# Attention of a two-layer block in the order of a list scheduler, without the repeated products at its begin

## The chip, the core and the metric

The kernel runs on one core of a Trainium2 chip. The core has TensorE (PE, matrix products into PSUM), VectorE (DVE), ScalarE (ACT), GpSimd (POOL) and SyncE (SP, which here only issues DMAs). Each engine works through its own queue in order; semaphores join them. The metric is the device time of one execution in microseconds, the median of the runs shown.

## What is computed

The reference is a two-layer block on x of shape 16 x 128 x 32 x 32, all in float32. The change touches layer 0 alone: linear attention, then the input side of a spectral filter.

```python
# --- layer 0 ---
x = x + _L0_conv_ref(_ln_c(x), ...)            # linear attention over 1024 tokens, 4 heads
t = _to_tokens(x)
t = t + _L0_ffn_ref(_ln_t(t), ...)             # causal FFT convolution with 16 filters, and taps
x = _from_tokens(t, x)
# --- layer 1: convolution block, then routed experts ---
...
# inside the attention:
q = softmax(q, over tokens) * SCALE
k = softmax(k, over channels of a head)
context = einsum('bhdc,bhec->bhde', k, v)
out = einsum('bhde,bhdc->bhec', context, q)
# inside the filter, per sample: three taps
out = out + einsum('btd,de->bte', u shifted by i, Mu[i])
```

## The kernel before

The 16 samples of x, 512 KB each, pass through the core in stages. The first, lines 221 to 774, is the attention stage; the second (L777 on) generates transfer matrices and multiplies spectra; then come layer 1's convolution and experts. Only the attention stage is edited.

**One sample in the attention stage** is some sixty named steps, methods of the class `Attention` (L356 on). In order of dependence:

- `tokens` (L367): issues the load of sample b + 2, then eight PE transposes of x into a PSUM tile. `moments` (L378, statistics on DVE at L135), `tokens_copy` (L374, ACT), `variance`, `root` (ACT: logarithm and exponential, L121 and L122), `scales` (one Newton step on DVE, L127 to L129, and the shift, L390), `norm` (L407, eight ACT operations at L144), `spread`, `group`, `group_var`, `group_root`, `group_scale` for the group norm.
- `channels` (PE transposes back, L172), `channels_copy` (ACT, gives xn), `q_` and `k` (PE, L433 and L451), the two softmaxes (`q_max`, `k_max`, `k_sub`, `k_sum` on DVE; `q_exp`, `k_exp` on ACT; `k_scale` on POOL, L476), `q_tokens`, `q_copy`, `context` (L499), `context_mask`, `fold` and `fold2` with their copies, `out` (L534), `out_add` (DVE, L539, adds to x).
- `input` (L543, PE transposes of the new x at L157), `moments2`, `input_copy` (ACT, L550, gives ub), `variance2`, `root2`, `scales2`, `norm2` (ACT, L144), then three users of ub: `even` and `odd` (PE, L571: half of the spectrum each) and `taps_in` (PE, L172). Behind `even` and `odd` stand ACT copies (L245, L247), DVE sums (L254 to L267) and POOL butterflies (L285 to L309), the last of them in `odd_turns4` (L625), which also issues the spectrum's write to DRAM (`vd`, L628). Behind `taps_in` stand `taps_copy` (ACT, gives u), `taps` (L633, twelve products at L639) and `taps_add` (L645, DVE at L646), which issues the write of x (`xd`, L647).

A float32 product appears in the profile as two PE instructions, a transpose as one.

**Set-up work** is woven in. `filters` (L649) makes the filters' spectra (`ph`) out of `phi` and `wf` (products at L657) and mixes sixteen 512 KB pieces `mi` into `mst` on DVE (L686, L688). `prepare` (L692) scales convolution weights on POOL.

**PSUM.** All 1024-column tiles come from `big()` (L343), three buffers in turn: a step that opens one waits until the third-last has been read. Small ones come from the tag `s`, two buffers.

**What sets the order.** PE, DVE, ACT and POOL run exactly in the order of the program text (`manual_schedule` with `PINNED`, L46 and L759); SP is not pinned in this stage. The order is written out by hand: the tuple `period` (L742) lists the steps with how many periods each runs behind `taps_in`; the loop over p (L760) goes through it once per period for 16 + 6 periods, so that steps of up to seven samples are interleaved. `filters` and `prepare` are generators that advance one piece per period.

**Repeated products.** `keep` (L159) multiplies the identity by itself into an unused tile. In this stage the table `idle` (L354) places 5, 4, 1 and 2 of them at the begin of the program.

**Planner.** `planned` (L1783) is a list scheduler that the layer-1 stage already uses: from a table of steps (engine, cost in us, due time, what it depends on, which buffers it opens and closes) it makes one order. Among the steps that can start within 0.25 us of the earliest, it takes the one with the earliest due time.

**After the stage** (L873 on, SP pinned too) four reads `xc` of chunk 0 (L793) feed POOL's `turns` (L808, L809), `generate` (L817) and its copies `g` on DVE and ACT (L828, L830), then `multiply` (L841).

## Time and profile before

| | us |
|---|---|
| median of 3 runs (lowest, highest) | 1227.47 (1225.88, 1232.86) |
| the profiled execution, device time | 1229.05 |
| its span, first to last instruction | 1227.0 |
| first product on x (PE, L152) | 7.53 |
| start of the first, eleventh and last `taps` | 87.54, 303.55, 378.78 |
| end of the last spectrum's butterflies (POOL) | 386.66 |
| first full run of products at L841 | 399.54 |

| busy in the span | us | share |
|---|---|---|
| PE | 1155.2 | 94% |
| DVE | 932.7 | 76% |
| ACT | 721.2 | 59% |
| POOL | 602.2 | 49% |

The page's groups give, for each line and engine, the count of instructions, their busy time and mean, and the idle time in front of them with what ended most of it. The answers on waits put that idle time down to pairs of lines. The chain of waits goes back from the last instruction, at each step to what released it. A matmul's end is modelled and overlaps the next one, so work on PE is best read from the distance between starts. The mean granted clock of TensorE was 0.988.

### The profile page before, as it was taken

To read this page: it belongs to the slowest core of one execution; us is meant where nothing else is said; L and a number is where in the kernel's file an instruction comes from. 1 tells how busy PE (TensorE), PEld (TensorE's weight loads), DVE (VectorE), ACT (ScalarE), POOL (GpSimd) and SP (SyncE) were. 2 spreads that over 40 slices of the span, in tenths; PEclk is the share of its full clock that TensorE was granted. 3 is DMA by queue.
4 is the path that set the end of the run, shared out by engine and by line. 5 is a ranking of instruction groups with operands and counts; after the bars stand their busy time and mean duration, and the time that the engine had idled before them with its cause. 6 is when DMAs were issued, how large, how long until landed. Compare 5 with 4: busy or idle time off the path is not lost.

```text
span 1227.0 us, 34351 instructions
## 1 busy us (share of the span) xinstructions
PE 1155.2 (94%) x14364; PEld 946.8 (77%) x14364; DVE 932.7 (76%) x1956; ACT 721.2 (59%) x1414; POOL 602.2 (49%) x800
## 2 busy tenths in 40 slices
PE   6889999999999999999997999999999999998996
PEld 4677767777677899998996888888888888885453
DVE  5888888887767677777764689898888989877335
ACT  4777777776656777877760445555555555554211
POOL 2436454664568788888882433343333333230003
PEclk9999999999999999999998999999999999999998
DMA  7004435243446244344348511233233322416998
GB/s 283 24 31 158 133 99 173 87 160 124 132 142 182 81 141 139 137 139 140 125 147 282 134 52 52 87 103 120 80 121 112 103 86 70 155 35 237 357 404 341
DMA packets 91243, 175.14 MB, mean 143 GB/s; under 512 B 5968, under 2 KB 42064, under 8 KB 90448
## 3 DMA queue, kind: packets, MB, share of 16 engines
q1 hardware_dynamic: 90448, 170.46, 41.1%
q0 software_dynamic: 640, 2.49, 0.6%
q8 instruction: 113, 1.85, 0.6%
q14 instruction: 42, 0.34, 0.1%
HBM read 110.28 MB, written 62.65 MB: 141 GB/s over the span
## 4 chain that ended last, share of the span: by engine, by line
PE 52%; DVE 22%; issue 10%; ACT 5%; DMA 5%; POOL 5%; SPq 0%; POOLq 0%; DVEq 0%; ACTq 0%
PE pcv L1013 10%; PE py L841 8%; PE pg L817 8%; PE big L639 6%; DVE bst L135 4%; PE big L172 3%; PE big L152 3%; PE big L571 3%; PE big L451 2%; PE big L534 2%; PE big L433 2%; DVE abss L1256 1%; DVE xp L1278 1%; DVE xp L1140 1%; POOL v L808 1%
## 5 line engine op out<-in xcount | busy, mean ns | idle before, releaser
L1013 PE MATMUL pcv<-v,cw 128*128 128x256 f32 x1152 | 258.2, 380 | 1.6 <-POOL v L1203 1.6
L1013 PEld LDWEIGHTS pcv<-v,cw 128*128 128x128 f32 x1152 | 214.7, 190 | 34.7 <-issue 4.9
L828 DVE COPY g<-pg 128x512 f32<-128x512 f32 x196 | 127.6, 682 | 67.9 <-PE pg L817 67.9
L830 ACT COPY g<-pg 128x512 f32<-128x512 f32 x316 | 161.1, 606 | 28.7 <-PE pg L817 27.9
L817 PE MATMUL pg<-ph,mst 32*128 32x128 f32 x4096 | 138.9, 278 | 1.4 <-DVE x L646 0.9
L817 PEld LDWEIGHTS pg<-ph,mst 32*128 32x128 f32 x4096 | 125.9, 187 | 15.6 <-DVE g L828 8.3
L841 PE MATMUL py<-g,v 128*32 128x128 f32 x4096 | 126.0, 276 | 1.9 <-POOL v L809 1.6
L841 PEld LDWEIGHTS py<-g,v 128*32 128x32 f32 x4096 | 109.2, 110 | 9.7 <-POOL v L809 2.1
L144 ACT ACTIVATE tok<-tok,sts 128x128 f32<-128x128 f32 x256 | 101.9, 480 | 16.9 <-DVE sts L1090 13.6
L135 DVE BATCH_NORM_STATS2 bst<-big 128x6 f32<-128x256 f32 x252 | 89.6, 416 | 19.9 <-PE big L152 10.7
L808 POOL TENSOR_TENSOR v<-xc 128x256 f32<-128x256 f32 x128 | 98.0, 790 | 9.9 <-DMA xc<-vd 9.2
L639 PE MATMUL big<-u,mu 128*128 128x128 f32 (+4 forms) x384 | 86.0, 380 | 0.0
L1203 POOL TENSOR_TENSOR v<-abss 128x256 f32<-128x256 f32 x64 | 49.1, 787 | 68.2 <-DVE abss L1199 56.8
L287 POOL TENSOR_TENSOR xf<-ab 128x256 f32<-128x256 f32 x34 | 24.8, 728 | 112.6 <-DVE ab L254 112.5
L1222 POOL TENSOR_TENSOR yo<-abss 128x256 f32<-128x256 f32 x32 | 23.5, 734 | 107.5 <-DVE abss L1218 107.5
L639 PEld LDWEIGHTS big<-u,mu 128*128 128x128 f32 x384 | 56.7, 191 | 18.0 <-issue 15.4
L571 PE MATMUL big<-wf,ub 128*128 128x256 f32 x256 | 63.5, 392 | 0.2
L809 POOL TENSOR_SCALAR v<-v 128x256 f32<-128x256 f32 x64 | 55.0, 860 | 5.6
L476 POOL TENSOR_TENSOR ke<-ke,ks 128x1024 f32<-128x1024 f32 x16 | 30.6, 1913 | 54.9 <-DVE qs L484 43.2
L144 ACT ACTIVATE tt<-tt,sts 128x128 f32<-128x128 f32 x120 | 47.8, 481 | 13.9 <-DVE sts L1090 13.9
L571 PEld LDWEIGHTS big<-wf,ub 128*128 128x128 f32 x256 | 47.0, 193 | 9.1 <-ACT xn L424 3.0
L915 ACT COPY yt<-py 128x512 f32<-128x512 f32 x60 | 35.1, 585 | 31.2 <-ACT g L830 17.6
(277 smaller groups left out, 2479.8 us busy)
## 6 DMA issues: line engine op xcount, KB each, us to landing
we<-in_weight SPq DMA_DIRECT2D x32, 1024.0 KB, 9.1
xc<-vd SPq DMA_DIRECT2D x64, 256.0 KB, 3.0
yd<-ys SPq DMA_DIRECT2D x32, 512.0 KB, 3.6
vd<-xf SPq DMA_DIRECT2D x15, 1024.0 KB, 5.1
y<-yd SPq DMA_DIRECT2D x15, 896.0 KB, 6.1
x<-in_x SPq DMA_DIRECT2D x16, 512.0 KB, 5.5
mi<-in_M_phi SPq DMA_DIRECT2D x16, 512.0 KB, 4.7
xd<-x SPq DMA_DIRECT2D x16, 512.0 KB, 6.2
```

What stands on the lines that cost most here:

```text
L135: nc.vector.bn_stats(bst[:, j : j + 2, :].rearrange("p j s -> p (j s)"), src[:, j : j + 2, :].rearrange("p j c -> p c j"),)
L144: nc.scalar.activation(dst[:, j, :], src[:, j, :], AF.Identity, bias=nm[:, j : j + 1], scale=r[:, j : j + 1],)
L571: nc.tensor.matmul(dst, self.ub[:, q, :], wf[:, q, :], start=True, stop=True)
L639: nc.tensor.matmul(self.pa[:, a:hi], mu[:, NF - 1 - si, tap, :], self.u[:, a - tap : hi - tap], start=(tap == 0), stop=(tap == KU - 1),)
L808: nc.gpsimd.tensor_tensor(vv[:, x, 1:, bs], e, o, op)
L809: nc.gpsimd.tensor_scalar(v[:, :, 0, bs], v[:, :, 2, bs], -1.0, None, ALU.mult)
L817: nc.tensor.matmul(pg[r][:, i], mst[rs, 4 * q + i, :], ph[rs, c, :], start=True, stop=True,)
L828: nc.vector.tensor_copy(dst, src)
L830: nc.scalar.copy(dst, src)
L841: nc.tensor.matmul(py[rows, x, kl, :], v[:, (x * NM + m) * JL + jl, 1 - ri : 3 - ri, :] .rearrange("p k b -> p (k b)"), g[:, ((x * 2 + ri) ...
L1013: nc.tensor.matmul(pc[:, i], wt[:, dy, k, :], v[:, k, dy * WT : dy * WT + HT], start=(dy == 0), stop=(dy == 2),)
L1203: nc.gpsimd.tensor_tensor(v[:, k, WT : WT + HT], self.ab[:, 0], self.ab[:, 1], op)
```

## The change

1. The hand-written `period` goes. A table of 63 steps of a sample and 70 set-up steps, with costs, due times, dependences and buffers, is given to `planned`, and the loop issues the steps in the order that comes back. Loads and stores are steps of SP in the table, but the store and spectrum writes are still issued where `taps_add` and the new step `spec` stand.
2. `filters` becomes the class `Filters`, with the same operations cut into steps; `prepare` yields at more places.
3. The first eight samples' x are loaded before the stage, two, two, two and two around `wf` and `phi`; later ones as steps of their own.
4. `keep` at the begin of the program: 0 instead of 12 products.
5. `tokens_copy` and `input_copy` are cut into two halves.
6. For the last sample, the spectrum of chunk 0 leaves by SP, the other chunks' spectra and x by ACT's queue.
7. The stage's pools wait tile by tile when their memory is reused (`reuse_waits="tile"`); small tiles have 7 buffers instead of 5.

```diff
@@ pools
-            setup = a0.enter_context(tc.tile_pool(name="setup", bufs=2))
-            work = a0.enter_context(tc.tile_pool(name="awork", bufs=2))
+            setup = a0.enter_context(tc.tile_pool(name="setup", bufs=2, reuse_waits="tile"))
+            work = a0.enter_context(tc.tile_pool(name="awork", bufs=2, reuse_waits="tile"))
...
@@ small tiles, repeated products
-                return work.tile(shape, F32, name=name, tag=name, bufs=5)
+                return work.tile(shape, F32, name=name, tag=name, bufs=7)
-            idle = {("tokens", 1): 5, ("filters", 0): 4, ("channels", 0): 1, ("k", 1): 2}
+            idle = {("begin", 0): 0}
...
@@ tokens
-                    if self.b + 2 < B:
-                        load(self.b + 2)
...
@@ tokens_copy, and input_copy likewise
-                    nc.scalar.copy(self.tok, self.pt)
+                    for h in range(2):
+                        js = slice(h * NT // 2, (h + 1) * NT // 2)
+                        nc.scalar.copy(self.tok[:, js], self.pt[:, js])
...
@@ last spectra and x
+                def spec(self):
                     for cs in (slice(0, 1), slice(1, NCH)) if self.b + 1 == B else (slice(NCH),):
-                        nc.sync.dma_start(
+                        (nc.scalar if cs.start == 1 else nc.sync).dma_start(
...
-                    nc.sync.dma_start(xd[self.b], self.x)
+                    (nc.sync if self.b + 1 < B else nc.scalar).dma_start(xd[self.b], self.x)
...
@@ filters
+            class Filters:
...
+                def copies(self, parity):
+                    pe = self.kept[parity][0]
+                    t = class_copy(pe, 1)
+                    self.kept[parity] += [t, class_copy(pe, ROT) if parity else t]
...
+                def fetch(self, k):
+                    m, i = divmod(k, NF)
+                    self.mi = getattr(self, "mi", {})
+                    self.mi[k] = setup.tile([P, MB, C], F32, name="mi", tag="mi")
+                    nc.sync.dma_start(self.mi[k], io["M_phi"][i, :, m * MB : (m + 1) * MB, :])
...
@@ loads, table, loop
+            for b in range(2, 4):
+                load(b)
             nc.sync.dma_start(wf, io["wf"])
+            for b in range(4, 6):
+                load(b)
             phi = spool.tile([P, NQ, 2, P], F32, name="phi", tag="xf")
             nc.sync.dma_start(phi, io["phi"])
-            period = (
-                ("q_max", 3), ("out_add", 1), ("tokens", 6), ("moments", 6), ("context", 2),
...
+            for b in range(6, 8):
+                load(b)
+            table = (
+                ("load", "SP", 1.28, 2153.3, "", "x", ""),
+                ("tokens", "PE", 0.88, 4110.1, "load", "big:t tok", ""),
+                ("moments", "DVE", 1.337, -1802.8, "tokens~.6", "", "big:t"),
...
+                ("even", "PE", 1.73, 3523, "norm2~1.5", "big:e", "ub"),
...
+                ("spec", "SP", 2.6, -1380.7, "odd_turns4 odd_turns2 odd_turns even_turns2", "", "xf"),
+                ("taps_in", "PE", 0.93, 1350.6, "norm2~.7", "big:ti", "ub"),
+                ("taps_copy", "ACT", 0.934, 3637.8, "taps_in", "u", "big:ti"),
+                ("taps", "PE", 5.22, 6831.9, "taps_copy", "big:ta", "u"),
+                ("taps_add", "DVE", 1.147, 655, "taps input", "", "big:ta"),
...
+            buffers = dict(x=8, big=3, s=2, tok=3, xn=3, qe=2, ke=2, qt=2, cx=2, wy=2, wt=2, ub=2, et=2, er=1, ab0=2, ab1=2, xf=2, sd=2, u=2, mi=2)
...
+            order = planned(
+                table, buffers, B, 520.01, lambda b, name: b > 0 and name[:2] in ("f_", "p_"),
+                lambda b, name: START.get((b, name), START.get(name, 0.0)),
+            )
+            samples, setting, preparing = {}, Filters(), prepare()
             with tc.manual_schedule(engines=PINNED):
-                for p in range(-reach, B):
...
+                keep(ps, "s", idle["begin", 0])
+                for b, name in order:
...
+                    elif name == "load":
+                        if b >= 8:
+                            load(b)
+                    elif name != "store":
+                        if name == "tokens":
+                            samples[b] = Attention(b)
+                        getattr(samples[b], "q_" if name == "q" else name)()
+                    keep(ps, "s", idle.get((name, b), 0))
```

## The prediction

> **What bounds the kernel now.** I read the page first. TensorE (PE) is busy for 94% of the span, but a busy PE is not a full one, so I looked for its waits by stretch. The attention stage ends where the first generated product stands (L817, 384.08 us), and only this stage is edited. Next came PE's waits, first from 75 to 330 us, then from 7 to 75 us (columns: total us, times, longest):
> ```profile
> PE big L172 <- ACT ub L550: 9.9, 12, 1.6
> ...
> PE pw L524 <- DVE wy L519: 3.4, 2, 2.7
> ```
> In the middle one wait recurs every sample. The chain of waits shows it inside one period (start, us, what):
> ```profile
> 207.90 1.44 DVE bst L135 x4
> ...
> 209.41 1.02 ACT ub L550
> ...
> 210.48 1.09 PE big L172 x8
> ...
> 216.47 5.21 PE big L639 x24
> ```
> From the end of `input` (L157) the chain leaves PE for `moments2` on VectorE (DVE) and the copy on ScalarE (ACT). PE had one other job to fill it, half the spectrum products (207.93 to 209.67), and idles 0.8 us. `taps` (L639) starts at 195.14, 216.47 and 237.79: a period of 21.33 us, about 20.5 of it PE's own work.
>
> Third, stretches cut at my landmarks: the end of the first `taps` (92.6), the start of the eleventh (about 303.5, cut at 309), the end of the last (384.0):
> ```profile
> 7.50:92.60 85.10, 75.08 (x471) 55.07 (x472) 65.96 (x192) 57.61 (x119) 29.30 (x37) 0.98 0.29 107
> 92.60:309.00 216.40, 207.71 (x1416) 158.65 (x1415) 178.94 (x426) 158.29 (x330) 118.21 (x182) 0.99 0.41 132
> ```
> The columns are length, then PE, weight load, DVE, ACT and POOL with instruction counts, clock, DMA. In the first stretch DVE is 78% busy, and 10.96 us of PE's busy time are repeated products of the identity (L165). So the start is bound by neither engine but by the order in which each waits for the other; the middle is bound by PE plus the one wait.
>
> **Start (until the first `taps` ends).** The change drops the 24 instructions of L165, 0.43 us apart, 10.3 us of PE. They stand in waits (10.83, 19.61, 26.89, 42.43 us), so by themselves they give nothing. What counts is the new order. Adding up each queue of the changed program with durations from the rows, less 0.07 us of overlap on DVE: up to the first `taps_add`, DVE has 64.2 us of work (now 62.2, done in 84.5) and PE has 60.6 (now 66.8 with the repeated products). DVE alone, starting at 9.54, would allow 73.7.
> Following the queues: `phi` now has four more x tiles in front, 2.1 MB at the 410 to 430 GB/s of this stretch, 5 us: it lands at about 21 instead of 15.95. PE's queue has eight filter products (16 instructions) in front of `k` of sample 0; until then PE has only short work. [...] Rows:
> ```profile
> 7.53 3.46 PE L152 MATMUL big<-ident,x 128*128 128x128 f32 x16 [0.59 <-DMA x<-in_x]
> 10.83 4.46 PE L165 MATMUL wm<-ident 128*128 128x512 f32 x10
> ...
> 67.29 0.49 PE L524 MATMUL pw<-wy,wv 128*128 128x128 f32 x2 [2.71 <-DVE wy L519]
> 67.61 2.66 PE L451 MATMUL big<-wqk,xn 128*128 128x128 f32 x16
> ```
> The first 16 transposes take 0.216 us each, later ones 0.11 (eight in 0.9): half speed. After a 2.71 us gap, `k` took 2.66 instead of 1.95. [...] By the row at 67.61 a drop costs some 1.3 (0.7 on `k`, 0.6 on the products of L433). I take 1.7 once: filter products 21 to 26.2, `k` until 28 (now it starts at 29.22). DVE's queue from `k_max` to `moments2` of sample 0 holds 22 us, because three samples' `k` and `q` are brought forward into it; with 2 us of waits `input` of sample 0 stands at 52.3 (now 62.27). From there PE has 30 us to the end of `taps`, DVE 24.9 beside it. I add 10%: 85 instead of 92.6, **7.6 saved**. Ends: 74 (DVE dense) and 93 (nothing gained).
>
> **Middle (start of the first `taps` to that of the eleventh): now 216.0 us.** In the new PE queue of a steady period, `input` is followed by one fold, `tokens`, `k`, `q`, `taps` and `out`, 12 us, before `taps_in` needs the normalized tokens. The chain needs: `moments2` 1.43, copies 1.15, roots 0.55, newton 1.5, eight normalizations 3.2, some 8.3 with hops, and 9.5 with the other sample's copies and roots between. The 0.8 us wait goes. What is late next? Each of the three `big` buffers must come free in order. Tightest: `odd` to `tokens` (copy, two scaled sums: 2.2 against 3.0 of PE work), and `taps` to `even` (DVE's `k_sum` and `taps_add` behind ACT's exponential: about 0.6 us of slack). All fit, barely. By fixed spacings (0.86 us a pair of 512 columns, and so on down) PE's queue holds 197.6 us between those two `taps`; the same sum gives 19.8 for a period whose measured work is 20.5, so 203.5. In the first five periods DVE has 18.3 to 21.7 us each, the filter mixing included, as much as PE: I add 3. **206.5, 9.5 saved.** Ends: 203 and 216.
>
> **Tail (to the end of the last `taps`): now 75.3 plus 5.2.** PE's queue holds 65.3 by spacings, 67.3 as measured. For the last three samples only `taps` (5.2) covers the norm chain of the next; its eighth normalization comes about 1.6 us later than dense work would want it: 3 x 1.6. **72.1, 3.2 saved.** Ends: 68 and 76.
>
> **Hand-over.** The chain of waits behind the last butterfly:
> ```profile
> 386.68 4.87 DMA vd<-xf
> 391.61 5.45 DMA xc<-vd
> ...
> 397.13 1.43 POOL v L808 x2
> ```
> and SP's own queue:
> ```profile
> 380.43 6.07 SPq L793 DMA_DIRECT2D xc<-vd  x3
> 386.68 0.80 SPq L628 DMA_DIRECT2D vd<-xf  x2
> 387.56 3.65 SPq L647 DMA_DIRECT2D xd<-x  x1
> 391.61 2.39 SPq L793 DMA_DIRECT2D xc<-vd  x4
> ```
> Three reads of chunk 0 stand ahead of the last spectrum's write, the fourth behind a 3.65 us issue. Moving the rest of the spectra and x to ACT's queue clears that issue. [...] But in the new program order all four reads stand behind the small write on SP. They then land from 3.5 us after the last butterfly (3.0 median landing) instead of before it, and POOL's four turns, 2.27 each, end at about 12.6 to 13.4 after it; now the main products start 12.9 after it. ACT gets two issues: x before the last butterfly, the spectra after. Behind them wait ACT's sixteen `g` copies; but DVE's already wait for that last butterfly in both programs, so ACT loses only the issue, 0.4 to 0.8 us. No ACT issue stands in the trace: between nothing and 3.65, nearest SP's 0.37 to 0.80. Generation then ends at about 11.2, still ahead of the turns. **0.4 lost** (ends: 1.5 gained, 4 lost).
>
> x loads no longer queue with `tokens`, halved copies add 32 instructions at about 0.1 us on ACT (61% to 73% busy: hidden under PE; uncovered 3 us). Tile-wise reuse of buffers and seven small ones take waits away that ended earlier anyway: nothing, the most a fraction of a microsecond at the hand-over.
>
> **Sum:** 7.6 + 9.5 + 3.2 - 0.4 = 19.9 from the profiled execution's 1229.05 (span 1227.0): 1209.1. The median shown, 1227.47, is 1.6 below that execution: **1208**. About 6 us (0.5%) either way is what a measurement can tell from no change.
>
> **Rivals.**
> 1. *Dense from the start.* DVE and PE hardly wait for each other: `taps` ends at 79, middle 204, tail 69; 31 saved, 1197. For it: the hand-check shows no late buffer. Against it: DVE is at PE's load in five periods. 0.20.
> 2. *The start gives nothing.* Without the repeated products PE falls to half speed more than once, and `taps` stays near 92: 12 saved, 1216. For it: the 0.216 us transposes. Against it: DVE's queue fills up with three samples. 0.14.
> 3. *Hand-over collision.* ACT's issue blocks for 3.65 and the reads share the engines with 1 MB of spectra: 4 more, 1212. 0.06.
> 4. *Slower: a late buffer in every period.* `even` takes the buffer that `taps` leaves only with `taps_add`; on DVE that stands behind `k_sum`, which waits for ACT's `k_exp` behind the normalizations, some 12.3 us after `input` where PE comes at 12.9. Should the chain take 14.2 us, the 1.3 a period over 15 periods eats the whole gain; at 14.6 it is 1.7 a period, 25.5 against the 19.9 gained, and 1208 becomes 1234. What could stretch it: small operations vary, the 128x8 multiply at L128 took 0.17 us at 216.33 and 0.59 at 213.68. Against it: it needs 2.3 us more than the rows add up to. 0.06.
> That the change doesn't reorder is excluded: the built queues show it.
>
> The forecast itself has 0.54, with its own range 1201 to 1215. The range 1194 to 1220 leaves out the slow rival and the extremes. Faster 0.90, same 0.04, slower 0.06.
>
> **What would show it.** The wait `L172 <- ACT ub` gone; `taps` every 20.4 us in the middle; first `taps` ending at 85; last at 364; filter products cold; reads of chunk 0 landing after the last butterfly. A period of 21.3 or more with a new wait, on `taps_add` or `k_sub`, would make me wrong; so would a first `taps` beyond 92.

## The result, and the profile after

Before: 1227.7 us in the median of 20 runs (1224.04 to 1237.89). After: 1224.29 us in 20 (1220.24 to 1228.34). The ratio is 0.9959, 95% interval 0.9941 to 0.9976: 0.4% faster. The forecast was 1208, its range 1194 to 1220, so the result lies outside it. The profiled execution took 1221.78 us (span 1219.6), 7.3 less than the one of before. Cut at the prediction's landmarks (both programs read from TensorE's timeline, which has the starts of the first and the eleventh `taps` 0.16 us earlier than the table of before):

| stage | before, us | after, us | saved | forecast |
|---|---|---|---|---|
| until the first `taps` starts | 87.4 | 84.7 | 2.7 | 7.6 |
| first to eleventh `taps` | 216.0 | 212.5 | 3.5 | 9.5 |
| to the end of the last `taps` | 80.8 | 75.6 | 5.2 | 3.2 |
| to the first full run of main products (L841, now L1011) | 15.4 | 17.8 | -2.4 | -0.4 |
| to the end | 827.5 | 829.0 | -1.5 | 0 |

What was to be seen: the wait that recurred every sample is gone. TensorE's waits from 75 to 330 us in the changed kernel (total, times, longest):
```profile
PE pg L402 <- DVE gt L398: 2.2, 1, 2.2
PE big L157 <- DVE ab L267: 1.3, 1, 1.3
PE big L573 <- DVE x L650: 1.0, 1, 1.0
PE pw L524 <- DVE wy L519: 0.9, 2, 0.6
```
`L172 <- ACT ub`, 9.9 us in 12 waits, is not in the list; what is left are single waits, and the largest are for VectorE. Where before the chain of waits left TensorE in each period for `moments2` and the copy `ub`, it now stays there (start, us, what):
```profile
243.73 0.93 PE big L172 x8
244.66 1.73 PE big L573 x8
246.39 0.87 PE big L152 x8
247.26 1.73 PE big L573 x8
248.99 1.08 PE pc L499 x32
...
256.90 5.21 PE big L643 x24
```
Nothing but products, without a gap: in the second half of the middle `taps` (now L643) follows itself every 20.21 us, where 20.4 was forecast. Not so in the first half. Stretches from the first `taps` on, cut at `taps`: limits, length, then PE, weight load, DVE, ACT, POOL with instruction counts, clock, DMA:
```profile
126.71:147.70 20.99, 19.45 (x108) 14.38 (x106) 19.78 (x42) 16.11 (x35) 6.81 (x14) 1.00 0.64 201
147.70:171.04 23.34, 21.17 (x167) 16.80 (x167) 20.65 (x45) 16.27 (x36) 13.01 (x20) 0.93 0.50 158
171.04:195.11 24.07, 23.14 (x151) 17.11 (x151) 23.31 (x52) 16.64 (x38) 11.41 (x19) 1.00 0.55 176
195.11:216.31 21.20, 20.86 (x147) 16.35 (x146) 20.39 (x47) 16.34 (x36) 9.57 (x16) 1.00 0.33 101
216.31:236.52 20.21, 20.21 (x143) 15.87 (x142) 16.33 (x43) 16.25 (x36) 9.62 (x16) 1.00 0.34 104
```
Two things differ between the first four rows and the last: DVE has 3.5 to 7 us more, and PE's own work is uneven, up to 23.1 us in one period. In the second row the granted clock is 0.93 besides.

In the start, VectorE's small operations have grown. The timeline of DVE, and that of POOL beside it (start, us, engine, line, operation):
```profile
38.01 0.93 DVE L128 SCALAR_TENSOR_TENSOR ga<-ga 128x1 f32<-128x1 f32 x1
38.97 0.92 DVE L129 SCALAR_TENSOR_TENSOR ga<-ga 128x1 f32<-128x1 f32 x1
39.92 0.16 DVE L416 TENSOR_TENSOR ga<-ga,vecs 128x1 f32<-128x1 f32 x1
...
73.85 1.90 DVE L129 SCALAR_TENSOR_TENSOR ga<-ga 128x1 f32<-128x1 f32 x1
```
```profile
37.92 1.00 POOL L733 TENSOR_TENSOR pcw<-pcw,raw 128x384 f32<-128x384 f32 x1
38.88 1.00 POOL L734 TENSOR_TENSOR pcw<-pcw,raw 128x384 f32<-128x384 f32 x1
...
73.82 1.91 POOL L476 TENSOR_TENSOR ke<-ke,ks 128x1024 f32<-128x1024 f32 x1
```
With one number per lane, such an operation takes 0.16 us where no POOL instruction began before it (third row). The others end each time when a POOL instruction ends: 38.94 beside 38.92, 39.89 beside 39.88, 75.75 beside 75.73. L733 and L734 are steps of `prepare`, the scaling of convolution weights, of which each period did one before; L476 is `k_scale`. The planner put 18.7 and 19.9 us of POOL's work between 25 and 50 and between 50 and 75 us, where it was 5.1 and 11.7. Take the operations on at most eight numbers per lane that last more than 0.25 us, and add up what each has above 0.17 us: this excess is 13.1 us up to 90 us (10.8 and 11.5 in two more executions of the changed kernel), and 21 of the 22 operations end within 0.06 us of the end of a POOL instruction. Before the change it was 4.3.

At the hand-over the chain of waits now reads:
```profile
374.24 0.32 SPq L632
...
374.66 6.40 DMA xc<-vd
...
381.19 1.43 POOL v L978 x2
...
390.58 1.49 PE py L1011 x21
```
SP sends the small slice at the last butterfly's end and only then the reads of chunk 0; the first lands 6.4 us after its issue, and POOL's four turns of 2.3 us stand behind it. In the queue view ACT's two issues took 0.36 and 0.40 us, far from the 3.65 that SP's had taken. TensorE waits 2.46 us for the turns before the first eight main products and 1.17 behind them, and what follows runs slowly:
```profile
390.58 3.21 PE L1011 MATMUL py<-g,v 128*32 128x128 f32 x56 [1.17 <-POOL v L979]
393.72 3.16 PE L987 MATMUL pg<-ph,mst 32*128 32x128 f32 x64
396.81 1.96 PE L1011 MATMUL py<-g,v 128*32 128x128 f32 x64
```
64 products of generation take 3.16 us here and 2.07 a little later. In the 20 us from the first main product on, the granted clock is 0.83; before the change it was 0.91, behind waits of 0.33 and 1.20 us. So the hand-over is best read up to the 65th instruction of the main products, where work flows again: 24.0 us behind the last `taps` here, 20.7 before.

### The profile page after: what moved, and what is told of

Read it like the earlier page. It is cut to its first block, busy times and chain, and to the rows that moved or that the text cites. A ratio compares the mean times of both kernels' runs of the same rounds, so it can differ in the third digit from the quotient of the medians.

```text
span 1219.6 us, 34402 instructions
## 1 busy us (share of the span) xinstructions
PE 1148.9 (94%) x14340; PEld 945.8 (78%) x14340; DVE 943.6 (77%) x1956; ACT 726.9 (60%) x1446; POOL 603.6 (49%) x800
## 4 chain that ended last, share of the span: by engine, by line
PE 42%; DVE 27%; issue 11%; POOL 8%; ACT 5%; DMA 5%; SPq 0%; POOLq 0%; DVEq 0%; ACTq 0%
PE pcv L1183 10%; PE py L1011 7%; PE pg L987 7%; DVE bst L135 4%; PE big L573 3%; PE big L152 3%; POOL v L978 3%; PE big L172 3%; PE big L643 3%; POOL v L979 2%; DVE abss L1426 1%; PE big L534 1%; DVE xp L1448 1%; DVE xp L1310 1%; PE big L451 1%
## 5 line engine op out<-in xcount | busy, mean ns | idle before, releaser
L987 PEld LDWEIGHTS pg<-ph,mst 32*128 32x128 f32 x4096 | 126.7, 188 | 16.4 <-DVE g L998 7.8
L1011 PE MATMUL py<-g,v 128*32 128x128 f32 x4096 | 126.2, 276 | 3.9 <-POOL v L978 2.5
L1011 PEld LDWEIGHTS py<-g,v 128*32 128x32 f32 x4096 | 109.1, 111 | 12.0 <-POOL v L978 2.6
L643 PE MATMUL big<-u,mu 128*128 128x128 f32 (+4 forms) x384 | 86.2, 381 | 0.0
L643 PEld LDWEIGHTS big<-u,mu 128*128 128x128 f32 x384 | 57.3, 191 | 23.8 <-issue 15.8
L476 POOL TENSOR_TENSOR ke<-ke,ks 128x1024 f32<-128x1024 f32 x16 | 30.6, 1914 | 72.3 <-DVE qs L484 42.6
L573 PEld LDWEIGHTS big<-wf,ub 128*128 128x128 f32 x256 | 45.9, 192 | 15.4 <-ACT ub L144 7.9
L287 POOL TENSOR_TENSOR xf<-ab 128x256 f32<-128x256 f32 x34 | 25.2, 742 | 64.3 <-DVE ab L254 64.2
L144 ACT ACTIVATE ub<-ub,sts 128x128 f32<-128x128 f32 x128 | 50.8, 479 | 8.9 <-DVE sts L566 8.9
```

The lines of the kernel that those rows point to most:

```text
L144: nc.scalar.activation(dst[:, j, :], src[:, j, :], AF.Identity, bias=nm[:, j : j + 1], scale=r[:, j : j + 1],)
L573: nc.tensor.matmul(dst, self.ub[:, q, :], wf[:, q, :], start=True, stop=True)
L643: nc.tensor.matmul(self.pa[:, a:hi], mu[:, NF - 1 - si, tap, :], self.u[:, a - tap : hi - tap], start=(tap == 0), stop=(tap == KU - 1),)
L987: nc.tensor.matmul(pg[r][:, i], mst[rs, 4 * q + i, :], ph[rs, c, :], start=True, stop=True,)
L1011: nc.tensor.matmul(py[rows, x, kl, :], v[:, (x * NM + m) * JL + jl, 1 - ri : 3 - ri, :] .rearrange("p k b -> p (k b)"), g[:, ((x * 2 + ri) ...
```

## Experiments

Four theories. **A**: POOL's early preparation stretches VectorE's small operations, and that costs the start. **D**: in the middle, VectorE's filter mixings cost the long periods (rival **E**: PE's own work and its order do). **F**: at the hand-over the reads behind the small slice cost the time (rival **G**: the data in flight, or generation). **H**: the start loses by half rate, because the repeated products are gone. Against A stands **S**: the stretched operations only change places, and cost in the middle what they save in the start. Times are medians; each ratio is to the kernel before, run beside it. Landmarks are those of the one profiled execution: start of the first `taps`, start of the eleventh, end of the last, first main product (its first eight, where they come ahead of the full run), and the 65th instruction of the main products.

| run | first | eleventh | last ends | main | 65th | median us | ratio, interval |
|---|---|---|---|---|---|---|---|
| before | 87.4 | 303.4 | 384.2 | 397.9 | 404.8 | 1227.7 to 1231.0 |  |
| changed | 84.7 | 297.2 | 372.8 | 389.0 | 396.8 | 1224.3 | 0.9959, 0.9941-0.9976 |
| changed, again | 84.3 | 298.5 | 374.1 | 390.6 | 397.9 | 1225.9 | 0.9983, 0.9959-1.0007 |
| changed, third | 83.7 | 297.4 | 373.0 | 389.7 | 396.9 | 1224.1 | 0.9943, 0.9917-0.9970 |
| prepare late, 1 | 80.3 | 296.8 | 375.4 | 391.9 | 399.9 | 1222.7 | 0.9959, 0.9944-0.9974 |
| mixing spread | 82.7 | 295.0 | 373.5 | 391.2 | 399.1 | 1226.6 | 0.9978, 0.9962-0.9993 |
| both | 80.0 | 297.7 | 377.7 | 396.6 | 404.4 | 1228.0 | 0.9990, 0.9971-1.0010 |
| slice by ACT | 83.9 | 297.6 | 373.2 | 387.2 | 391.0 | 1219.5 | 0.9915, 0.9891-0.9940 |
| all by SP | 83.7 | 297.6 | 373.3 | 392.0 | 398.9 | 1224.1 | 0.9955, 0.9930-0.9980 |
| repeated products | 83.3 | 293.3 | 369.0 | 385.0 | 392.5 | 1224.5 | 0.9967, 0.9940-0.9994 |
| few mixings | 84.2 | 294.2 | 369.9 | 385.7 | 392.6 | 1216.7 | 0.9898, 0.9844-0.9951 |
| before, prepare early | 101.6 | 314.0 | 394.8 | 408.4 | 412.3 | 1240.7 | 1.0091, 1.0057-1.0124 |
| pools, copies undone | 83.9 | 297.7 | 373.5 | 390.3 | 397.2 | 1223.6 | 0.9977, 0.9954-1.0000 |
| prepare late, 2 | 79.8 | 310.7 | 386.7 | 403.2 | 411.0 | 1236.3 | 1.0081, 1.0057-1.0106 |
| late 2 + slice + repeated | 79.9 | 311.4 | 387.4 | 401.3 | 405.2 | 1234.4 | 1.0061, 1.0037-1.0085 |
| prepare late, 3 | 80.8 | 294.1 | 370.7 | 387.2 | 395.1 | 1217.6 | 0.9907, 0.9871-0.9942 |
| slice by ACT, again | 83.6 | 295.0 | 370.6 | 384.6 | 388.5 | 1213.6 | 0.9874, 0.9838-0.9910 |
| slice + repeated | 84.6 | 296.9 | 372.6 | 389.0 | 392.8 | 1221.8 | 0.9939, 0.9911-0.9966 |
| slice + repeated + late 3 | 80.2 | 292.0 | 368.0 | 381.9 | 385.7 | 1214.9 | 0.9887, 0.9850-0.9923 |
| slice + late 3 | 80.4 | 293.2 | 369.0 | 383.6 | 387.4 | 1213.0 | 0.9842, 0.9808-0.9877 |

The changed kernel ran twice more beside these. The last `taps` and the first main product of the second execution came 1.3 and 1.6 us later than those of the first, where 1 us had been expected: so much is scatter.

**Prepare late, 1 (theory A).** In the planned order, everything else stays:
```diff
+moved = [k for k in order if k[1][:2] == "p_"]
+order = [k for k in order if k[1][:2] != "p_"]
+for b in range(5, B - 1):
+    at = order.index((b, "taps")) + 1
+    order[at:at] = [moved.pop(0) for _ in range(min(3, len(moved)))]
...
```


> The changed kernel, with only the steps that prepare convolution weights on POOL taken out of their planned places (all before the third `taps`) and put behind `taps` of samples 5 to 13, three at a time; the rest of the order is untouched. Theory A (POOL's early preparation stretches VectorE's small operations, 13.1 us of excess over 0.17 us each up to 90 us against 4.3 before the change): the excess in that stretch falls below 6 us, the first `taps` starts at 77 to 81 instead of 84.7, the program ends 4 to 8 us earlier than the changed kernel, 1216 to 1220, unless a later wait takes it back. Rival B (the start is limited by TensorE's cold clock and by the order itself): the excess falls, but the first `taps` stays at 83 to 86 and the time at 1223 to 1225. Rival C (small operations are stretched by something other than POOL): the excess stays at 11 to 14 us.

The excess fell from 13.1 to 5.5 us and the first `taps` came at 80.3, 4.4 us earlier. From 7.5 us to the first `taps`, after and in this run:
```profile
7.50:84.66 77.16, 66.61 (x459) 51.43 (x459) 70.39 (x180) 54.40 (x119) 48.19 (x52) 1.00 0.41 150
```
```profile
7.50:80.28 72.78, 65.76 (x459) 51.48 (x459) 63.40 (x179) 54.07 (x118) 21.12 (x30) 1.00 0.32 122
```
Nearly the same instructions, but DVE is busy 7.0 us less and POOL 27. A holds for the start. The time hardly followed (median 1222.7): the last `taps` ended at 375.4, later than in the changed kernel. TensorE's waits from the first to the eleventh `taps` of this run name the largest piece of what took the gain back:
```profile
PE pc L499 <- POOL ke L476: 3.3, 1, 3.3
```
Three steps in a row stood ahead of `k_scale` in POOL's queue.

**Mixing spread, and both moves (theory D).** One mixing a sample, as before the change:
```diff
+order = [k for k in order if k[1][:4] != "f_ld" and k[1][:3] != "f_m"]
+for k in range(NF * EPR // MB):
+    at = order.index((k, "taps")) + 1
+    lds = ["f_ld0", "f_ld1"] if k == 0 else [f"f_ld{k + 1}"] if k + 1 < NF * EPR // MB else []
+    order[at:at] = [(0, n) for n in lds + [f"f_m{k}"]]
```


> The changed kernel, with only the sixteen mixings of filters on VectorE and their loads moved: one behind `taps` of each sample, as before the change, in place of fifteen of them by the sixth `taps`. Theory D (periods two to six are VectorE's, because of the mixings): these periods fall from 20.6 to 24.1 us to 20.2 to 21 each, the eleventh `taps` starts 5 to 9 us earlier than 297.2, the drop of the clock at 150 to 170 us goes, the time is 1215 to 1219. Rival E (the periods are long for want of a `big` buffer or by the order of TensorE's queue): the periods stay above 21 on average and the time at 1222 to 1225.

> Both moves together: preparation behind `taps` of samples 5 to 13 and one mixing a sample. If A and D both hold and are separate, the gains add: the last `taps` ends 9 to 15 us earlier than 372.6 and the time is 1209 to 1215. If only one of them carries, this equals the better of the two single moves. If VectorE is limited by its sum over the whole stage, the steady periods lengthen from 20.2 to 21 or more and the sum of the gains is at most 5 us.

The middle took 212.3 us instead of 212.5. The long periods, 23.3 and 24.1 in the changed kernel, still took 22.0 and 22.7, and the short ones grew from 20.2 to between 20.3 and 20.8: so a mixing costs TensorE up to 0.6 us in a full period too. Both moves together were the worst of these (median 1228.0), with periods of 21.8 to 23.0. D falls in the form that I gave it.

**Few mixings.** Twelve of sixteen left out:
```diff
+order = [k for k in order if not (k[1][:4] == "f_ld" or k[1][:3] == "f_m") or int(k[1].lstrip("f_ldm")) % NF == 0]
```


> The changed kernel, leaving out twelve of the sixteen mixings of filters and their loads (the filters then hold one basis each, and later stages compute with that). It takes about 14 us of VectorE's work away instead of moving it. Theory D2 (VectorE's work as a whole sets periods two to six, and moving it only moved the wait): the eleventh `taps` starts 6 to 9 us earlier than 297.2, and the last ends as much earlier. Theory E (the order of TensorE's queue and its own work set them): it starts at 295 to 297, less than 2.5 us earlier, with the waits at the same places.

The middle shrank by 2.4 us, to 210.1, for some 14 us of VectorE's work. That sum hides two things. The first period, in which the changed kernel has no mixing, took 24.2 us here and 20.8 to 23.0 in the other executions of this order, because eight products ran at half rate behind a wait:
```profile
94.47 3.59 PE L573 MATMUL big<-wf,ub 128*128 128x256 f32 x8 [1.54 <-DVE x L650]
```
They take 1.99 us in the other executions. And the changed kernel's middle has a spell of half rate of its own (the row with clock 0.93). Periods two to six, where the mixings stood, took 105.1 us here, against 108.4 and 108.5 in the two runs that have all mixings in the planned order and kept a clock of 1.00 in the middle (repeated products, and slice by ACT again). So the mixings are worth 3.4 us: more than E's bound of 2.5, and well below D's 6 to 9. Three quarters of the work taken away are hidden beside TensorE. The median, 1216.7 of only four executions, lies 7.6 us below the changed kernel's, where the 65th instruction comes 4.2 earlier; the difference stays open. From about the first to the eleventh `taps`:
```profile
84.20:294.20 210.00, 205.69 (x1421) 159.69 (x1421) 175.52 (x427) 162.77 (x351) 109.39 (x178) 0.99 0.34 108
```
Of 210.0 us PE is busy 205.7. In the changed kernel the same count is 206.3 of 212.5, and in the two runs at clock 1.00 it is 204.5 and 204.7. So E holds in the main: PE's own work sets a floor of some 204.5 us for the middle (an estimate from these counts), and the forecast had set 203.5.

**Slice by ACT, twice, and all by SP (theory F).**
```diff
-(nc.scalar if cs.start == 1 else nc.sync).dma_start(
+(nc.scalar if self.b + 1 == B else nc.sync).dma_start(
```


> The changed kernel, with the small slice of the last spectrum also sent by ScalarE's queue, so that SP's reads of chunk 0 no longer stand behind that write. Theory F (the hand-over lost 2.5 us and then 1.5 us of clock because the reads went out only after the last butterfly): three of the four reads land before the last butterfly ends, POOL turns begin with no wait, the first main product starts 14.5 to 16 us after the last `taps` ends instead of 18.0, TensorE's gap before it stays under 1.5 us and its clock there above 0.9: 2 to 4 us saved, 1220 to 1222. Rival G (the megabyte of spectra in flight makes the reads slow wherever they stand, or generation is what ends last): the first main product stays at 17 to 18.5 us behind the last `taps`, time 1223 to 1225.

> The changed kernel with the small slice of the last spectrum by ScalarE's queue, once more. Theory F: first main product 13.5 to 14.5 us behind the last `taps` (14.0 at the first look, 16.2 and 16.5 in the changed kernel), no wait of TensorE on `v` there, the clock not below 0.97 in the 100 us behind it, and the time 2 to 5 us under the changed kernel's 1224 to 1226: 1219 to 1223. If the first look's 1219.5 was scatter: 1223 to 1226.

Without the slice in SP's queue the reads no longer wait for the last butterfly. SP's queue in the first of these runs, and POOL's timeline:
```profile
365.94 15.43 SPq L963 DMA_DIRECT2D xc<-vd  x7
```
```profile
374.59 1.41 POOL L978 TENSOR_TENSOR v<-xc 128x256 f32<-128x256 f32 x2
...
383.57 1.43 POOL L978 TENSOR_TENSOR v<-xc 128x256 f32<-128x256 f32 x2 [1.97 <-DMA xc<-vd]
```
The first read goes out 8.7 us before the last butterfly ends, the first turn begins with no wait, and only the fourth waits, 1.97 us. The first main products stand 14.0 and 13.9 us behind the last `taps`, in one full run, against 16.2, 16.5 and 16.6 in the three executions of the changed kernel; no wait on `v` is left there, and the clock in this gap is 1.00. More still comes behind the first main product, where there is now neither a wait nor half rate. The second of the two runs:
```profile
384.57 1.96 PE L1011 MATMUL py<-g,v 128*32 128x128 f32 x64
386.45 2.07 PE L987 MATMUL pg<-ph,mst 32*128 32x128 f32 x64
```
The 65th instruction of the main products comes 17.8 us behind the last `taps` in both, against 24.0, 23.8 and 23.9: 6 us, where 2 to 4 were expected. The ratios, 0.9915 and 0.9874, lie below all three intervals of the changed kernel. F is shown.

All by SP, the move of the queue undone:
```diff
-(nc.scalar if cs.start == 1 else nc.sync).dma_start(
+nc.sync.dma_start(
...
-(nc.sync if self.b + 1 < B else nc.scalar).dma_start(xd[self.b], self.x)
+nc.sync.dma_start(xd[self.b], self.x)
```


> The changed kernel with the last sample's other spectra and its x sent by SP again, all else unchanged: what the move of the queue is worth in the new order. Theory F (the reads of chunk 0 decide the hand-over, and on SP they stand behind whatever is issued there): the reads go out behind the issue of x, 3.65 us before the change, and of the spectra, so the first main product starts about 4 us later than in the changed kernel, and the time is 1226 to 1229. Rival G (moving the queue is worth nothing, for generation ends last or the engines are shared anyway): within 1 us of 1224.

The main products came 18.7 us behind the last `taps`, 2.1 to 2.5 later than in the three executions of the changed kernel, and the 65th instruction 1.6 to 1.8 later: the issue of x took 1.60 us here, not 3.65. The median, 1224.1, doesn't show this; its interval is 6 us wide. So F's mechanism held, its size (4 us) was too large, and in the new order the move of the queue is worth about 2 us by the trace.

**Repeated products (theory H).**
```diff
-idle = {("begin", 0): 0}
+idle = {("begin", 0): 0, ("tokens", 1): 2, ("tokens", 2): 6}
```


> The changed kernel with repeated products put back into the two early waits of TensorE, two behind `tokens` of sample 1 and six behind `tokens` of sample 2. Theory H (the cold clock at 18 to 24 us costs the start 1.3 us or more): the filter products take 3.5 us instead of 4.5, the first `taps` starts 1 to 2.5 us earlier than 84.7, the time is 1222 to 1223.5. Theory A (VectorE, stretched by POOL, sets the start): the products are faster, but the first `taps` stays at 84 to 85.5 and the time at 1224 within 1.5.

The filter products took 3.53 us (21.18 to 24.71), as expected, and `k` of sample 0 started 1.66 us earlier; the first `taps` came at 83.3, in the second run with this edit (slice + repeated) at 84.6. Without the edit the changed kernel's three executions have 83.7 to 84.7. Nothing is gained at the start: VectorE is what it waits for (of TensorE's waits from 5 to 85 us, without the 5.7 at the begin, 4.3 are for VectorE, 1.6 for ACT and 1.2 for loads). The last `taps` at 369.0 did not repeat either (372.6).

**Before, prepare early: the mirror.**
```diff
-                    next(preparing, None)
+                    for _ in range(1 if p >= 0 else 4):
+                        next(preparing, None)
```


> The kernel before, with only the preparation of convolution weights on POOL brought forward: four steps in each of the six periods ahead of the first `taps`, where there was one, and so nothing of it left behind. The mirror of the late preparation. Theory A (POOL's work stretches VectorE's small operations and the start waits for VectorE): the excess over 0.17 us each up to 90 us rises from 4.3 to 10 us or more, and the first `taps` starts 3 to 6 us later than 87.4; of that less than 2 us comes back in the middle, where POOL then is freer; 1229 to 1233. Rival B (the start is limited otherwise): first `taps` within 1.5 us of 87.4, time 1226 to 1229.

The direction came out, 11 us slower (1.0091), but by another road. The excess was 6.7 us only, where 10 had been expected. TensorE's waits from 5 to 95 us in this run have a first row that the kernel before doesn't have:
```profile
PE pc L499 <- POOL ke L476: 10.6, 1, 10.6
```
`k_scale` stood behind the preparation in POOL's queue. So the start of this run shows that early preparation is dear there, and says nothing for the stretched operations. Its middle does. It took 212.5 us instead of 216.0, and all of the difference lies in the two periods, 22.29 and 23.98 us long, in which the kernel before has three POOL operations of `prepare` (L720 to L722); without them both periods take 21.33. Before, in the second of them:
```profile
270.83 1.01 POOL L720 TENSOR_TENSOR pcw<-pcw 128x384 f32<-128x384 f32 x1
271.00 0.87 DVE L128 SCALAR_TENSOR_TENSOR ga<-ga 128x1 f32<-128x1 f32 x1
275.43 1.09 PE L172 MATMUL big<-ident,ub 128*128 128x128 f32 x8 [1.63 <-ACT ub L550]
276.53 3.48 PE L571 MATMUL big<-wf,ub 128*128 128x256 f32 x8
```
and in this run:
```profile
284.27 0.16 DVE L128 SCALAR_TENSOR_TENSOR ga<-ga 128x1 f32<-128x1 f32 x1
288.85 1.99 PE L571 MATMUL big<-wf,ub 128*128 128x256 f32 x8
```
The stretched operations (a second one, L416, took 0.85 us) delay `moments2` and the copy `ub`, TensorE waits 1.63 us instead of 0.66, and here half rate comes on top. The mechanism that cost the start stood in the trace of before.

**Prepare late, 2, alone and with two more edits.** Two steps behind the last turn of samples 1 to 13:
```diff
...
+for b in range(1, B - 2):
+    at = order.index((b, "odd_turns4")) + 1
+    order[at:at] = [moved.pop(0) for _ in range(min(2, len(moved)))]
...
```


> The changed kernel with the preparation on POOL moved once more, now two steps behind the last turn (`odd_turns4`) of samples 1 to 13, where POOL is free for 7.1 us of each steady period. In the late preparation of before, three steps in a row stood ahead of `k_scale` and TensorE waited 3.3 us for it once and 1.7 once. Theory A (POOL's early preparation costs the start 4 us, and the first late version gave it back at `k_scale`): the first `taps` starts at 80 to 81.5, the middle from there to the eleventh takes 212 to 214, the last `taps` ends at 368.5 to 371, 2 to 4 us before the changed kernel's. Theory S (VectorE's stretched operations only change places, and cost in the middle what they save in the start): the middle takes 215 or more and the last `taps` ends at 372 to 375.

> Three things together on the changed kernel: the small slice of the last spectrum by ScalarE's queue, repeated products in the two early waits, and the preparation two steps behind the last turn of each sample. If the savings add (about 3 at the start, 1.5 of clock, 2 to 5 at the hand-over): first `taps` at 78.5 to 81, last `taps` ending at 366 to 370, first main product 14 to 15 us behind it, time 1212 to 1217. If they don't add: 1218 to 1221, the value of the small slice alone.

Both failed in the same place, one period of 36 us. The first `taps` came at 79.8. Then, in SP's queue, in the chain of waits and on DVE of the first of the two:
```profile
176.55 0.33 SPq L721 DMA_DIRECT2D raw<-in_w  x1
178.32 0.38 SPq L632 DMA_DIRECT2D vd<-xf  x1
178.79 3.53 SPq L702 DMA_DIRECT2D mi<-in_M_phi  x2
```
```profile
178.79 8.28 DMA mi<-in_M_phi
```
```profile
187.10 0.75 DVE L708 TENSOR_SCALAR mst<-mi,coef 128x1024 f32<-128x1024 f32 x1 [10.25 <-DMA mi<-in_M_phi]
```
The load `raw` of the next preparation needs a buffer that POOL is still reading; SP waits for it, the filters' load `mi` waits behind `raw`, and the mixing that needs `mi` stands first in DVE's queue with all of the stage behind it. Of the 10.25 us that VectorE stood, 8.28 are the load's own time from issue to landing; it was issued too late to be hidden. Neither theory had foreseen this. It took 12 us and hid what the slice gives.

**Prepare late, 3, and the combinations.** Behind all filter loads, two steps behind a sample's last turn and one behind `k_scale`:
```diff
...
+for b in range(5, B - 1):
+    at = order.index((b, "odd_turns4")) + 1
+    order[at:at] = [moved.pop(0) for _ in range(min(2, len(moved)))]
+    if b + 4 < B and moved:
+        order.insert(order.index((b + 4, "k_scale")) + 1, moved.pop(0))
...
```


> The changed kernel with the preparation on POOL behind all filter loads: from sample 5 on, two steps behind the last turn of a sample and one behind `k_scale`. In the placement behind samples 1 to 13 a step's load on SP's queue waited for POOL, the loads of filters queued behind it, and VectorE stood 10.3 us before a mixing; here no filter load is left. Theory A (the start's 4 us are real and can be kept): first `taps` at 79.5 to 81, middle 212 to 214.5, last `taps` ending at 369 to 371.5, first main product 1.5 to 4 us before the changed kernel's 389 to 390.5. Theory S (VectorE's stretched operations only change places): last `taps` ending at 372 to 375.

> The small slice by ScalarE's queue, and repeated products in the two early waits of TensorE. Adds up, by the single looks: last `taps` ending at 368.5 to 370.5 (369.0 with the repeated products alone), first main product at 383 to 384.5, time 1216 to 1219. If the repeated products' 4 us were scatter of the looks: last `taps` at 372 to 374, time as with the slice alone.

> The small slice by ScalarE's queue, repeated products in the early waits, and the preparation behind the filter loads. If all three add: last `taps` ending at 365 to 368, first main product at 379 to 382, time 1212 to 1216, which would beat both kernels by 0.7% or more. By theory S the late preparation gives nothing on top: as with slice and repeated products alone, within 1 us.

First `taps` at 80.8, middle 213.3, last `taps` ending at 370.7, which is 2.1 to 3.4 us before the changed kernel's: A, as expected, and about two thirds of the 3 to 4 us of the start are kept. The steady periods are 20.3 to 20.6 instead of 20.2, and the excess of small operations between 90 and 300 us is 20.5 us instead of 10.6, so S has a share in it. Slice and repeated products together missed what was expected: the last `taps` ended at 372.6, and the first main product stood 16.4 us behind it. ACT's two spectrum writes took 2.53 us to issue (1.2 in the five other runs with the slice), TensorE waited 0.95 us for a copy of ACT's, and the clock in this gap was 0.90. Behind it nothing waits, and the 65th instruction comes 20.3 us behind the last `taps`: over half of the slice's saving is still there. With the late preparation it was 17.8, yet the median, 1214.9, is no better than the slice's second alone.

> The changed kernel with the small slice by ScalarE's queue and the preparation on POOL behind the filter loads, without repeated products. By theories A and F: first `taps` at 79.5 to 81, last `taps` ending at 368 to 371, first main product 13.8 to 16.5 us behind it (the upper end if the clock falls there), at 382 to 386, and the median 4 to 8 us below that of the changed kernel beside it. If the gains come from scatter between calls alone: less than 3 us below.

> The changed kernel as it is, as the partner of the run beside it: last `taps` ending at 371 to 374.5, first main product at 387.5 to 391, 1221 to 1226; the cold half rate behind the 2.2 us wait at about 156 us may or may not show.

Slice and late preparation together, side by side with the changed kernel: 1212.95 against 1224.11. It has the lowest ratio of all (0.9842 of before, 0.9808 to 0.9877) and beats both kernels. The first main product comes at 383.6 against 389.7, 6.1 us earlier, and the 65th instruction at 387.4 against 396.9, 9.5 earlier; the medians differ by 11.2. So most of the gain is placed. From there to the end the profiles of all runs, whatever their edit, took 820.1 to 831.5 us, so single microseconds can't be placed there. Part of this scatter is clock: the 110 executions of the kernel before that ran beside these runs took 1222.5 to 1239.7 us, and a straight line through them falls by 1.1 us for each 0.001 of mean granted clock (correlation -0.77).

**Pools and copies undone.**
```diff
-work = a0.enter_context(tc.tile_pool(name="awork", bufs=2, reuse_waits="tile"))
+work = a0.enter_context(tc.tile_pool(name="awork", bufs=2))
...
-                    for h in range(2):
-                        js = slice(h * NT // 2, (h + 1) * NT // 2)
-                        nc.scalar.copy(self.ub[:, js], self.pt[:, js])
+                    nc.scalar.copy(self.ub, self.pt)
```


> The changed kernel with the pools' buffer reuse as before (the option on six pools taken out) and the two halved copies of ScalarE whole again. The forecast counted both as nothing. If so, all landmarks within 1 us of the changed kernel's and the time 1222 to 1226. If reuse or halving carried part of the gain, the steady period is 20.5 or more instead of 20.2 and a wait of TensorE on ScalarE's `ub` or `tok` returns: 1226 to 1230.

All landmarks lie within 1.4 us of the first execution of the changed kernel and within 0.9 of the second, the steady period is 20.2, the time 1223.6. Both parts are worth nothing that can be measured, as forecast.

## Why the prediction was wrong

1. **The start, 7.6 forecast, 2.7 measured.** The step that failed is "DVE has 64.2 us of work": the queue was summed with durations from the rows of before, where POOL was busy for 5.1 us between 25 and 50 us and 11.7 between 50 and 75, not 18.7 and 19.9 as now. Added up in the same way from the changed kernel's own rows, each duration less 0.07 us, the queue up to the first `taps_add` is 73.9 us long (71.9 and 72.3 in two more executions), and 65.3 and 65.7 with the preparation late (the first and the third). I had costed each engine's queue by itself, and the moved POOL steps at nothing. The rows show what that left out: L128 and L129 on one number per lane took 0.93 and 1.90 us, until the POOL instruction beside them ended, and L128 takes 0.16 without one (before, at 207.02); a `TENSOR_SCALAR` on eight numbers (L382, at 27.36) took 0.85 in the same way, and a reduction that ran beside POOL throughout (52.93, `ks` from `ke`) kept 1.21. Why one is stretched and the other not, no run here shows. With the preparation out of the way the first `taps` starts at 79.8 to 80.8 in seven runs; the forecast, 85 for its end, is 79.8 for its start. The order was judged rightly, the stretching left out. Rival 4 had the sign of it in hand, L128 at 0.17 and at 0.59 us, and took it for variation; the long one ended at 214.27 us, and a POOL butterfly at 214.24.
2. **The filter products at half rate, forecast at 1.7 us once.** No run shows the 1.7. The products did begin at half rate, 0.43 us an instruction in the first four and 0.22 from the seventh on (the granted clock recorded from 20 to 26 us is 1.00 all the same), and took 4.53 us against 3.53 with repeated products ahead of them: 1.0 lost. But it was not on the path: the 3.53 gave nothing at the first `taps`. So rival 2's cause falls, though its size (a start that gives next to nothing) was nearer than mine.
3. **The middle, 9.5 forecast, 3.5 measured.** The mechanism held: the wait went, and the steady period is 20.21. Two terms were too small, and one was missing. PE's own work: 203.5 by spacings, 206.3 measured. Of these 2.8 us, 1.1 are a slip of the sum: 197.6 times 20.5 over 19.8 is 204.6, and the runs at clock 1.00 measured 204.5 and 204.7. The rest is a spell at half rate (granted clock 0.71 from 155 to 160 us), for which the middle had no term; the profile of before has one too (0.69 from 275 to 280). Waits: 3 forecast, 6.2 measured. The run with few mixings takes back 3.4 us over periods two to six. The rest are waits of the order itself, such as 2.2 us of `group` for `spread` and 1.3 of `input` for an odd sum, each once.
4. **The tail, 3.2 forecast, 5.2 measured.** No experiment bears on it, and its cause stays open.
5. **The hand-over, 0.4 lost by forecast, 2.4 measured.** The reads did stand behind the small slice, as forecast. The term that failed is "They then land from 3.5 us after the last butterfly (3.0 median landing)": the first landed 6.8 after it, with 1.5 MB of ACT's queue moving beside it (from 372 to 392 us that queue took 25.5% of the time of the 16 DMA engines and SP's 31.2%), and the turns ended 16.3 after it instead of 12.6 to 13.4. That looks like the second half of rival 3, which had 0.06, but no run takes the traffic away alone; its first half fell, for ACT's issue took 0.4 us. The gain was near: with the slice in ACT's queue too, three of four reads go out early, and 6 us come back.
6. **Behind it, 1.5 us more, not forecast.** From the first main product to the 65th instruction the changed kernel took 7.85 us and the one before 6.90: 0.95 of the 1.5, by half rate behind a longer wait. The forecast had no term for the clock there. The rest is within scatter.
7. **Rivals 1 and 4** fell: the start was not dense (10.6 of its 77.2 us PE is idle), and no wait for a late `big` buffer exists in steady periods.

The sum: 4.9 us missing at the start, 6.0 in the middle, 2.0 at the hand-over, 1.5 behind it, and 2.0 more than forecast in the tail: 12.4 of the forecast 19.9 are missing on the profiled executions. The medians differ by 3.4 only; three profiled executions of the changed program lie 6.8 us apart (1221.78 to 1228.57). The one used here had a granted clock of 0.988, above the mean of its 20 executions, 0.985; by the slope above that is some 3 us (an estimate), about what the median lies above it.

## What to carry to other kernels

A planned order moves work of engines that nobody waits for; cost it by what it does to the neighbours, the small operations of VectorE beside POOL first of all (0.16 us alone here, up to 1.90 beside it), and by what stands behind it in each in-order queue. Before a read is put behind a write, check whether it depends on that write: here a slice of 64 KB in SP's queue held back four reads, three of which needed none of it. Read a hand-over up to where work flows again, for here the first product showed under half of what the slice gives. And set the floor of a stage by an engine's measured busy time, not by ideal spacings.

## What the runs showed of the hardware that I had not expected

The same wait was followed by half rate of TensorE in one execution and not in the other. Slice + repeated products, and slice again:
```profile
155.85 0.38 PE L402 MATMUL pg<-gt,avg 128*128 128x1 f32 x2 [2.16 <-DVE gt L398]
156.09 3.17 PE L573 MATMUL big<-wf,ub 128*128 128x256 f32 x8
```
```profile
155.60 0.38 PE L402 MATMUL pg<-gt,avg 128*128 128x1 f32 x2 [2.15 <-DVE gt L398]
155.84 1.97 PE L573 MATMUL big<-wf,ub 128*128 128x256 f32 x8
```
After an idle time of 2.16 and 2.15 us eight products took 3.17 us and 1.97. In the changed kernel, where they took 3.04, the granted clock from 155 to 160 us is 0.71. Of thirteen profiled kernels that kept this order, nine show a period of 23.3 to 23.4 us there, as at half rate, and four of 22.1: one execution's landmarks carry 1.2 us of chance here. Half rate stood behind shorter waits too. In the profile of before, a wait of 1.63 us (the rows at 275.43) was followed by it (clock 0.69 from 275 to 280) and one of 1.62 us, at 103.84, was not (1.00 from 103 to 108); with few mixings 1.54 us was followed by it. Each of these waits has eight transposes right before or behind it; counted with them, and with the short product of `group`, TensorE was without longer products for 3.43 us (152.66 to 156.09, slice + repeated), 3.2 (few mixings) and 2.7 (before); but it was so just as long where full rate followed, 3.43 us in slice again (152.41 to 155.84) and 2.7 before the products at 104.95. What decides it no run here shows. And the price of an issue is not fixed: SP's issue of x, behind the same two writes, took 3.65 us before and 1.60 with everything on SP again, ACT's 0.35 to 0.36; and ACT's two spectrum writes took 1.2 us in five runs and 2.53 in one. What sets it stays open.
